# Gate and up products of the shared experts by Strassen's scheme, in an attention and mixture-of-experts block

## The chip, the cores and the metric

The kernel runs on one core of one Trainium2 chip. The metric is the device time of one launch in microseconds (us). Times of single instructions come from one profiled execution. The engines are called PE (TensorE, matrix products), DVE (VectorE), ACT (ScalarE), POOL (GpSimd) and SP (SyncE, which here only issues DMAs).

## The reference, cut to what matters

The program is one block of a transformer with adaptive layer norm: attention with 16 heads over 2048 tokens of width 512, then a feed-forward layer with 64 routed experts, four for each token, and two shared experts that see every token. All of it is float32. The change lies in the shared experts:

```python
h = _layernorm(x, axis=-1) * (1 + cb) + sb            # 2048 x 512, "flat" below
...
h = jax.nn.silu(jnp.einsum('ecd,edh->ech', xb, Wg)) * jnp.einsum('ecd,edh->ech', xb, Wu)
yb = jnp.einsum('ech,ehd->ecd', h, Wd)                # routed experts, 128 seats each
y = yb[eid, jnp.minimum(pos, CAP - 1)] * (w * valid)[:, None]
out = jnp.zeros((N, Dx), x.dtype).at[tok].add(y)
hs = jax.nn.silu(jnp.einsum('nd,sdh->nsh', flat, Sg)) * jnp.einsum('nd,sdh->nsh', flat, Su)
out = out + jnp.einsum('nsh,shd->nd', hs, Sd)         # shared experts: S = 2, HS = 512
```

Sg and Su have two shared experts of 512 hidden columns each, so 1024 hidden columns in all, over a width of 512.

## The kernel before, in words

The first two thirds of the time go to attention; nothing of it changes. After it the layer-normed tokens lie transposed in `h2T` (128 partitions, 4 chunks of the width, 2048 tokens), and the weights of the shared experts in `wsg` and `wsu`. `acc` holds the output, 16 tiles of 128 tokens.

The shared work is cut into 4 blocks `b` of 512 tokens and 8 chunks `i` of 128 hidden columns. One pair (b, i) is called a unit here. In `shared_up` a unit is two halves: the gate product and the up product, each four matmuls of 128x128 weights by 128x512 tokens, summed into one bank of PSUM (name `psg`, tag `gu`, three banks). After the second half `glu` makes silu(gate) times up: a sigmoid on ACT and two multiplies on DVE, and the result is `hs`. `shared_down` takes the eight `hs` of a block and makes the output of 128 tokens: eight matmuls of 512 columns and one add to `acc` on DVE.

The list `shared` holds all this in order: the units of a block, and after the first unit of the next block the four downs of the block before. It is used in three places, in an order written out by hand (`manual_schedule` keeps the order in which the program is written on each engine):

- The lead: the first `LEAD` = 9 halves, put between the last steps of the routing. The last of these steps writes `tok`, the table of which token sits in which expert's seat.
- The merged stage: the routed experts, step by step, are merged with the shared work by `merge`, which always takes from the list that is behind, by its columns of matmul work. For an expert, `expert_turn` transposes the gathered tokens (`load_xb` gathers them on POOL from `tok`), `expert_up` makes gate and up in one product (`pse`, also tag `gu`), `expert_mid` transposes the hidden values, and `expert_down` makes the output (`psy`), multiplies it by `gb` on DVE and writes it to memory (`ybd`). `load_expert` loads the three weights of an expert on SP's queue, into four buffers.
- The tail: the last `TAIL` = 26 entries of `shared`. Between them stands `combine`: for each tile of 128 tokens, four gathers on POOL fetch the outputs of its experts into `yg` (four buffers), and four multiply-adds on DVE put them into `acc`. `READY` sets the place of each combine by the columns of matmul work that stand before it, one tile for 3072 columns.

The tail ends with the four downs of the last block, each followed by a store of its tile.

Of the kernel before, what the change touches and what calls it, by code (L numbers as in the profile page):

```python
# [9 lines left out]
F32 = mybir.dt.float32  # L10
BF16 = mybir.dt.bfloat16
U32 = mybir.dt.uint32
AF = mybir.ActivationFunctionType
ALU = mybir.AluOpType
# [4 lines left out]
P = 128  # L19
# [4 lines left out]
def adaln_block_kernel(  # L24
# [23 lines left out]
    nc = tc.nc  # L48
    _, N, D = x.shape
    H, _, DH = Q_w.shape  # L50
    E, _, HE = Wg.shape
    S, _, HS = Sg.shape
# [4 lines left out]
    NB = N // 512  # L57
    NHC = S * HS // P
# [65 lines left out]
    with ExitStack() as att:  # L124
# [453 lines left out]
        left = []  # L578
# [362 lines left out]
    with ExitStack() as ex:  # L941
# [1 line left out]
        sgp = ex.enter_context(tc.tile_pool(name="sgp", bufs=2, side="right"))  # L943
        wdp = ex.enter_context(tc.tile_pool(name="wdp", bufs=1, side="right"))
        wts = ExitStack()
        ewp = wts.enter_context(tc.tile_pool(name="ewp", bufs=4, side="right"))
        wsd = wdp.tile([P, NHC, D], F32)
        hsh = {}
        weights = {}

        def load_expert(e):
            w = ewp.tile([P, DC, 2, HE], F32, name="wgu")
            nc.sync.dma_start(out=w[:, :, 0, :], in_=Wg[e].rearrange("(k p) h -> p k h", p=P))
            nc.sync.dma_start(out=w[:, :, 1, :], in_=Wu[e].rearrange("(k p) h -> p k h", p=P))
            wd = ewp.tile([P, D], F32, name="wd")
            nc.sync.dma_start(out=wd, in_=Wd[e])
            weights[e] = (w, wd)

        def glu(dst, pg, pu, width):

            sig = sgp.tile([P, 512], F32, name="sig")[:, :width]
            nc.scalar.activation(sig, pg, AF.Sigmoid)
            nc.vector.tensor_mul(sig, sig, pg)  # L963
            nc.vector.tensor_mul(dst, sig, pu)

        def shared_up(b, i):
            s, f = divmod(i, HS // P)
            parts = []

            def half(w):  # L970
                ps = psO.tile([P, 512], F32, name="psg", tag="gu", bufs=3)
                for k in range(DC):
                    nc.tensor.matmul(  # L973
                        out=ps,
                        lhsT=w[:, s, k, f * P : (f + 1) * P],
                        rhs=h2T[:, k, b * 512 : (b + 1) * 512],
                        start=(k == 0),
                        stop=(k == DC - 1),
                    )
                parts.append(ps)  # L980
                if len(parts) == 2:
                    hsh[b, i] = hsp.tile([P, 512], F32, name="hs")
                    glu(hsh[b, i], parts[0], parts[1], 512)

            return [(2048, lambda: half(wsg)), (2048, lambda: half(wsu))]

        def shared_down(b, i):
            t = 4 * b + i
            ps = psO.tile([P, D], F32, name="psd", tag="y")
            for f in range(NHC):  # L990
                nc.tensor.matmul(  # L991
                    out=ps,
                    lhsT=hsh[b, f][:, i * P : (i + 1) * P],
                    rhs=wsd[:, f, :],
                    start=(f == 0),
                    stop=(f == NHC - 1),
                )
            nc.vector.tensor_add(acc[:, t, :], acc[:, t, :], ps)
            if b == NB - 1:
                store(t)  # L1000
# [2 lines left out]
            nc.sync.dma_start(out=out[0, t * P : (t + 1) * P, :], in_=acc[:, t, :])  # L1003


        shared = []
        for b in range(NB):
            for i in range(NHC):
                shared += shared_up(b, i)
                if i == 0 and b > 0:  # L1010
                    shared += [(4096, lambda b=b, j=j: shared_down(b - 1, j)) for j in range(4)]
        shared += [(4096, lambda j=j: shared_down(NB - 1, j)) for j in range(4)]
        LEAD = 9
        TAIL = 4 + 2 * NHC + 4 + 2

        with tc.manual_schedule():
            nc.sync.dma_start(out=wsd, in_=Sd.rearrange("s (i p) d -> p (s i) d", p=P))
            for i in range(NHC):
                nc.gpsimd.tensor_mul(wsd[:, i, :], wsd[:, i, :], gb)
            for e in range(4):  # L1020
                load_expert(e)
            for n, (_, f) in enumerate(shared[:LEAD]):
                f()
                if n == 0:
                    turn_h(NT - 1)
                if n == 1:
                    seat_tokens(len(BLOCKS) - 2)
                if n == 1:
                    logit(NT - 1)
                    choice = choose(len(BLOCKS) - 1)  # L1030
                    next(choice)
                if n == 2:
                    next(choice)
                if n == 4:
                    positions(len(BLOCKS) - 1)
                if n == 6:
                    seat_tokens(len(BLOCKS) - 1)
        rts.close()
        xbp = ex.enter_context(tc.tile_pool(name="xbp", bufs=2))
        xbs = {}  # L1040
        xts = {}
        ups = {}
# [16 lines left out]
            nc.scalar.copy(xts[e], tp)  # L1059

        def expert_up(e):
            ps = psO.tile([P, 2 * HE], F32, name="pse", tag="gu", bufs=3)
            for k in range(DC):
                nc.tensor.matmul(  # L1064
                    out=ps,
                    lhsT=xts[e][:, k, :],
                    rhs=weights[e][0][:, k].rearrange("p i h -> p (i h)"),
                    start=(k == 0),
                    stop=(k == DC - 1),
                )  # L1070
            he = xbp.tile([CAP, HE], F32, name="he")
            glu(he, ps[:, :HE], ps[:, HE:], HE)
            ups[e] = he
# [6 lines left out]

        def expert_down(e):
            ps = psO.tile([CAP, D], F32, name="psy", tag="y")
            nc.tensor.matmul(out=ps, lhsT=hts[e], rhs=weights[e][1], start=True, stop=True)  # L1083
            y = xbp.tile([CAP, D], F32, name="y")
            nc.vector.tensor_mul(y, ps, gb)
            nc.scalar.dma_start(out=ybd[e * CAP : (e + 1) * CAP, :], in_=y)

        def expert_step(e):
            out = []

            def turn():
                if e + 3 < E:
                    load_xb(e + 3)
                expert_turn(e + 1)

            def down():
                expert_down(e - 2)
                if e + 2 < E:
                    load_expert(e + 2)

            if e + 1 < E:
                out.append((512, turn))
            if e < E:
                out.append((1024, lambda: expert_up(e)))
            if 0 <= e - 1 < E:
                out.append((128, lambda: expert_mid(e - 1)))
            if e >= 2:
                out.append((512, down))
            return out
# [22 lines left out]
        with tc.manual_schedule():  # L1132
            for e in range(3):
                load_xb(e)
            expert_turn(0)
            experts = []
            for e in range(E + 2):
                experts += expert_step(e)
            merge([experts, shared[LEAD:-TAIL]], [])
# [58 lines left out]
```

## Time and profile before

| | us |
|---|---|
| median of 3 runs | 2533.73 (2530.65 to 2536.56) |
| the profiled run | 2545.0 |
| its span | 2543.2 |
| PE, busy | 2445.4 |
| DVE, busy | 1431.6 |
| ACT, busy | 647.1 |
| the shared experts' gate and up matmuls (L973), busy | 235.4 |
| the shared experts' down matmuls (L991), busy | 111.5 |
| the routed experts' up matmuls (L1064), busy | 121.1 |
| the combines (L1126, DVE), busy | 47.8 |

The profiled run is one execution; its time stands beside its span because the rows of the trace add up to the span. "Busy" is the time in which an engine has at least one instruction in work; for PE the ends of the pipelined matmuls are modelled. A float32 matmul appears as two records of PE. The page cuts the span into 40 equal slices of 63.6 us, and gives in tenths how busy each engine is in each and what clock PE was granted. In a group's row stand the line, the engine, the operation, the tiles it writes and reads, the count, then the busy time, the mean of one in ns, and the idle time before it with what ended it. "Remote" or "unknown queue" as a releaser means that the trace doesn't show what ended a wait.

### The profile page before, as it was taken

The page shows a single profiled execution, that of the slowest core. Times are in us where ns is not written, and L with a number is a line of the kernel's source. Part 1 is how long each engine was busy: PE and PEld are TensorE (multiplying, and loading weights), DVE is VectorE, ACT ScalarE, POOL GpSimd, SP SyncE. Part 2 cuts the span into 40 slices and gives each one's busy share as a digit, 9 for nine tenths or more (in the row PEclk, how much of TensorE's full clock was granted, in tenths as well). Part 3 has the DMA queues.
Part 4 walks back from the last instruction along what each step waited for, and adds up shares of the span by engine and source line. Part 5 has one row for each costly group of instructions (what it writes and reads, how often), then busy time and mean ns, then how long its engine had stood idle before and what let it go on. Part 6 is the DMA issues. An engine that isn't in the chain of part 4 may idle for free.

```text
span 2543.2 us, 25501 instructions
## 1 busy us (share of the span) xinstructions
PE 2445.4 (96%) x8297; PEld 1484.3 (58%) x8297; DVE 1431.6 (56%) x2737; ACT 647.1 (25%) x1456; POOL 247.3 (10%) x306
## 2 busy tenths in 40 slices
PE   7999999999999999999999999989999999999989
PEld 4666666666666666666666666545444456566534
DVE  4566666666666666666666666663655522222354
ACT  3233323333232333323333333311111121211100
POOL 0000000000000000000000000040000211111163
PEclk9999999999999999999999999999999999999989
DMA  4234434444444343444444434564521467767564
GB/s 137 60 98 97 115 90 108 112 101 111 98 121 107 93 118 99 96 119 101 109 118 101 109 97 97 161 188 135 203 83 50 124 190 229 226 201 233 168 187 138
DMA packets 225420, 326.21 MB, mean 128 GB/s; under 512 B 32100, under 2 KB 140680, under 8 KB 225288
## 3 DMA queue, kind: packets, MB, share of 16 engines
q1 hardware_dynamic: 197960, 251.16, 38.2%
q0 software_dynamic: 18112, 56.64, 7.0%
q10 hardware_dynamic: 9216, 16.78, 1.7%
q8 instruction: 67, 1.10, 0.2%
q14 instruction: 65, 0.53, 0.1%
HBM read 139.91 MB, written 41.94 MB: 72 GB/s over the span
## 4 chain that ended last, share of the span: by engine, by line
PE 65%; DVE 18%; SPq 6%; issue 4%; DMA 4%; ACT 2%; another core or an unknown queue 1%; DVEq 0%; ACTq 0%; POOL 0%; POOLq 0%
PE pqk L169 12%; PE ps L408 12%; PE po L479 9%; PE psg L973 8%; DVE pt L461 6%; SPq L451 6%; PE pv L329 5%; PE pso L915 4%; PE pse L1064 4%; PE psd L991 4%; DVE nm L421 4%; DMA pt<-p 3%; DVE p L397 3%; PE psy L1083 2%; PE tpx L1057 1%
## 5 line engine op out<-in xcount | busy, mean ns | idle before, releaser
L427 ACT ACTIVATE p<-ps,nm 128x1024 f32<-128x1024 f32 (+7 forms) x384 | 332.2, 865 | 1041.4 <-DVE nm L425 368.5
L408 PE MATMUL ps<-kt,qt 128*128 128x512 f32 (+3 forms) x1280 | 536.6, 536 | 44.5 <-ACT p L427 43.6
L479 PE MATMUL po<-pt,v 128*128 128x256 f32 (+1 forms) x2304 | 568.2, 369 | 6.6 <-DVE pt L461 3.6
L479 PEld LDWEIGHTS po<-pt,v 128*128 128x128 f32 x2304 | 426.2, 191 | 221.7 <-issue 156.5
L421 DVE TENSOR_REDUCE nm<-ps 128x1 f32<-128x1024 f32 (+7 forms) x384 | 349.6, 910 | 92.2 <-PE ps L408 83.4
L461 DVE STREAM_TRANSPOSE pt<-pt 128x1664 f32<-128x1664 f32 (+2 forms) x160 | 318.0, 1988 | 66.3 <-DMA pt<-p 61.5
L408 PEld LDWEIGHTS ps<-kt,qt 128*128 128x128 f32 x1280 | 235.4, 191 | 195.4 <-issue 127.4
L420 DVE TENSOR_TENSOR ps<-ps,causal 128x128 f32<-128x128 f32 x256 | 74.5, 291 | 349.9 <-PE ps L408 349.9
L329 PE MATMUL pv<-wv,hT 128*128 128x256 f32 x1024 | 240.3, 379 | 0.0
L489 POOL DMA_DIRECT2D atd<-at x128 | 78.4, 613 | 1652.2 <-ACT at L488 1627.7
L169 PE MATMUL pqk<-hT,wq 128*128 128x512 f32 x512 | 231.5, 595 | 0.0
L169 PE MATMUL pqk<-hT,wk 128*128 128x512 f32 x512 | 231.2, 595 | 0.0
L397 DVE TENSOR_SCALAR p<-p,rs 128x1024 f32<-128x1024 f32 (+7 forms) x384 | 221.8, 606 | 9.3 <-DMA p<-atd 0.2
L329 PEld LDWEIGHTS pv<-wv,hT 128*128 128x128 f32 x1024 | 194.5, 190 | 31.4 <-issue 1.9
L915 PE MATMUL pso<-hT,v 128*128 128x512 f32 x384 | 175.5, 604 | 0.0
L169 PEld LDWEIGHTS pqk<-hT,wk 128*128 128x128 f32 x512 | 98.0, 192 | 102.3 <-issue 99.7
L169 PEld LDWEIGHTS pqk<-hT,wq 128*128 128x128 f32 x512 | 97.9, 191 | 97.3 <-issue 94.2
L973 PE MATMUL psg<-h2T,wsu 128*128 128x512 f32 x256 | 119.2, 610 | 10.4 <-DVE sig L963 10.4
L1064 PE MATMUL pse<-wgu,xbT 128*128 128x256 f32 x512 | 121.1, 379 | 0.0
L973 PE MATMUL psg<-h2T,wsg 128*128 128x512 f32 x256 | 116.2, 593 | 4.8 <-ACT h2T L750 2.8
L915 PEld LDWEIGHTS pso<-hT,v 128*128 128x128 f32 x384 | 70.7, 192 | 74.5 <-issue 73.7
L991 PE MATMUL psd<-wsd,hs 128*128 128x512 f32 x256 | 111.5, 592 | 0.0
(224 smaller groups left out, 1723.0 us busy)
## 6 DMA issues: line engine op xcount, KB each, us to landing
pt<-p SPq DMA_DIRECT2D x768, 104.0 KB
pt<-p SPq DMA_DIRECT2D x256, 124.0 KB
pt<-p SPq DMA_DIRECT2D x256, 108.0 KB
atd<-at POOLq DMA_DIRECT2D x128, 128.0 KB
wgu<-in_L_ffn_Wg_dram SPq DMA_DIRECT2D x64, 256.0 KB
wgu<-in_L_ffn_Wu_dram SPq DMA_DIRECT2D x64, 256.0 KB
wd<-in_L_ffn_Wd_dram SPq DMA_DIRECT2D x64, 256.0 KB
ybd<-y ACTq DMA_DIRECT2D x64, 256.0 KB
```

The costliest lines, as they stand in the source:

```text
L169: nc.tensor.matmul(out=ps, lhsT=w[:, k, :], rhs=hT[:, k, j * 512 : (j + 1) * 512], start=(k == 0), stop=(k == DC - 1),)
L329: nc.tensor.matmul(out=ps, lhsT=hT[:, k, t * P : (t + 1) * P], rhs=wv[:, k].rearrange("p i d -> p (i d)"), start=(k == 0), stop=(k == DC - 1),
L397: nc.vector.tensor_scalar(cols[:, :, a:b], cols[:, :, a:b], rs[:, n : n + 1], None, ALU.mult)
L408: nc.tensor.matmul(out=ps[:, o : o + wo], lhsT=q, rhs=kts[hd, (c0 + o) // 512][:, :wo], start=True, stop=True,)
L421: nc.vector.tensor_reduce(nm[:, n : n + 1], ps[:, :w], AX.X, ALU.max, negate=True)
L427: nc.scalar.activation(rows[:, r0 + c0 // P : r0 + (c0 + w) // P], ps[:, :w].rearrange("q (r b k) -> q r b k", b=4, k=32), AF.Exp, bias=nm ...
L461: nc.vector.transpose(part, part)
L479: nc.tensor.matmul(out=po if wide else po[:, P:], lhsT=vts[g][:, kt, hh * DH : (hh + 1) * DH], rhs=rows[:, r : r + last + 1 : last] if wid ...
L915: nc.tensor.matmul(out=ps, lhsT=abs_[pr][:, hd, i * P : (i + 1) * P], rhs=wo[:, hd, :], start=(hd == 0), stop=(hd == H - 1),)
L973: nc.tensor.matmul(out=ps, lhsT=w[:, s, k, f * P : (f + 1) * P], rhs=h2T[:, k, b * 512 : (b + 1) * 512], start=(k == 0), stop=(k == DC - 1),)
L991: nc.tensor.matmul(out=ps, lhsT=hsh[b, f][:, i * P : (i + 1) * P], rhs=wsd[:, f, :], start=(f == 0), stop=(f == NHC - 1),)
L1064: nc.tensor.matmul(out=ps, lhsT=xts[e][:, k, :], rhs=weights[e][0][:, k].rearrange("p i h -> p (i h)"), start=(k == 0), stop=(k == DC - 1),)
```

## The change

Gate and up of a unit, seen together, are a product of a 2 by 2 matrix of blocks with another one: the left factor has the rows gate and up and, as columns, the two halves of the width (256 each); the right factor has these two halves of the width as rows and two halves of the token block (256 tokens each) as columns. The plain way takes eight products of blocks. Strassen's scheme, in the form with shared sums, takes seven, of sums of blocks: four sums of weight blocks (`weight_sum`, per unit), four sums of token blocks (`token_sum`, per block of tokens), and seven sums of the products. All these sums are made on DVE, except one copy of a product, on ACT.

A unit is now four entries of the list, `first` to `fourth`, with two, two, two and one products. Each product is two matmuls of 256 columns, and two products share one bank of PSUM. The multiplies of `glu` move to `first` of the next unit. The first four units, in the lead, stay as they were; `LEAD` is 8 entries, and `TAIL` now holds eleven units where it held nine. The experts' `pse` leaves the tag `gu` for `pl`, which has one bank. The experts' weights are loaded by two functions into three buffers each, `load_up` right after the product that reads the buffer, and `load_down` where all three were loaded before. The tokens' sums of odd blocks go into tiles that are no longer used (`ga`, `cb`, `sb`, `parts[0]`).

```diff
-        ewp = wts.enter_context(tc.tile_pool(name="ewp", bufs=4, side="right"))
+        ewp = wts.enter_context(tc.tile_pool(name="ewp", bufs=3, side="right"))
...
-        def load_expert(e):
+        def load_up(e):
             w = ewp.tile([P, DC, 2, HE], F32, name="wgu")
             nc.sync.dma_start(out=w[:, :, 0, :], in_=Wg[e].rearrange("(k p) h -> p k h", p=P))
             nc.sync.dma_start(out=w[:, :, 1, :], in_=Wu[e].rearrange("(k p) h -> p k h", p=P))
-            wd = ewp.tile([P, D], F32, name="wd")
-            nc.sync.dma_start(out=wd, in_=Wd[e])
-            weights[e] = (w, wd)
+            weights[e] = w
+
+        def load_down(e):
+            downs[e] = ewp.tile([P, D], F32, name="wd")
+            nc.sync.dma_start(out=downs[e], in_=Wd[e])
...
+        HB = 256
...
+        def token_sum(b, j):
+
+            def quad(k, n):
+                return h2T[:, 2 * k : 2 * k + 2, b * 512 + n * HB : b * 512 + (n + 1) * HB]
...
+            if b % 2 == 0:
+                dst = tsp.tile([P, 2, HB], F32, name=f"ts{j}")
+            else:
+                dst = (ga, cb, sb, parts[0])[j - 1].rearrange("p (k n) -> p k n", k=2)
...
+            if j == 1:
+                nc.vector.tensor_sub(dst, quad(0, 1), quad(0, 0))
+            elif j == 2:
+                nc.vector.tensor_sub(dst, quad(1, 1), ts["1"])
+            elif j == 3:
+                nc.vector.tensor_sub(dst, quad(1, 1), quad(0, 1))
+            else:
+                nc.vector.tensor_sub(dst, quad(1, 0), ts["2"])
...
+        def weight_sum(n, j):
...
+            dst = wsp.tile([P, 2, P], F32, name=f"ws{j}")
+            a, b, op = {
+                1: ("21", "22", ALU.add), 2: ("1", "11", ALU.subtract),
+                3: ("11", "21", ALU.subtract), 4: ("12", "2", ALU.subtract),
+            }[j]
+            nc.vector.tensor_tensor(dst, left[a], left[b], op)
...
+        FACTORS = {
+            1: ("11", "11"), 2: ("12", "21"), 3: ("4", "22"), 4: ("22", "4"),
+            5: ("1", "1"), 6: ("2", "2"), 7: ("3", "3"),
+        }
+
+        def products(n, js):
+            ps = psO.tile([P, 2, HB], F32, name="pst", tag="gu", bufs=3)
+            for h, j in enumerate(js):
+                left, right = FACTORS[j]
+                w, x_ = units[n][left], tsets[UNITS[n][0]][right]
+                for k in range(2):
+                    nc.tensor.matmul(
+                        out=ps[:, h], lhsT=w[:, k, :], rhs=x_[:, k, :],
+                        start=k == 0, stop=k == 1,
+                    )
+            return [ps[:, h] for h in range(len(js))]
+
+        def first(n):
+            u = unit(n)
+            p1, p6 = products(n, (1, 6))
+            u["p1"] = sgp.tile([P, HB], F32, name="p1")
+            nc.scalar.copy(u["p1"], p1)
+            u["u"] = sgp.tile([P, HB], F32, name="u", bufs=1)
+            nc.vector.tensor_add(u["u"], u["p1"], p6)
+            while glus:
+                glus.pop()()
+
+        def second(n):
+            u = units[n]
+            p7, p5 = products(n, (7, 5))
+            u["v"] = sgp.tile([P, HB], F32, name="v", bufs=1)
+            nc.vector.tensor_add(u["v"], u["u"], p7)
...
+            nc.vector.tensor_add(u["up"][:, HB:], u["v"], p5)
+            nc.vector.tensor_add(u["u"], u["u"], p5)
+            for j in (1, 2, 3):
+                weight_sum(n + 1, j)
+
+        def third(n):
+            u = units[n]
+            p4, p3 = products(n, (4, 3))
+            nc.vector.tensor_add(u["up"][:, :HB], u["v"], p4)
+            nc.vector.tensor_add(u["g"][:, HB:], u["u"], p3)
+            weight_sum(n + 1, 4)
+
+        def fourth(n):
+            u = units[n]
+            (p2,) = products(n, (2,))
+            nc.vector.tensor_add(u["g"][:, :HB], u["p1"], p2)
+            sig = sgp.tile([P, 512], F32, name="sig512")
+            nc.scalar.activation(sig, u["g"], AF.Sigmoid)
...
+            def finish():
+                nc.vector.tensor_mul(sig, sig, u["g"])
+                nc.vector.tensor_mul(hsh[b, i], sig, u["up"])
+
+            glus.append(finish)
+            if b + 1 < NB:
+                for j in {4: (1, 2), 5: (3,), 6: (4,)}.get(i, ()):
+                    token_sum(b + 1, j)
...
+        LEAD = 8
         shared = []
...
+        for i in range(LEAD // 2):
+            shared += shared_up(0, i)
+        UNITS = [(b, i) for b in range(NB) for i in range(NHC)][LEAD // 2 :]
+        for n, (b, i) in enumerate(UNITS):
+            for c, f in ((1024, first), (1024, second), (1024, third), (512, fourth)):
+                shared.append((c, lambda n=n, f=f: f(n)))
+            if i == 0 and b > 0:
+                shared += [(4096, lambda b=b, j=j: shared_down(b - 1, j)) for j in range(4)]
         shared += [(4096, lambda j=j: shared_down(NB - 1, j)) for j in range(4)]
-        LEAD = 9
-        TAIL = 4 + 2 * NHC + 4 + 2
+        TAIL = 4 + 4 * NHC + 4 + 12
...
-            for e in range(4):
-                load_expert(e)
+            for e in range(3):
+                load_up(e)
+                load_down(e)
...
-            ps = psO.tile([P, 2 * HE], F32, name="pse", tag="gu", bufs=3)
+            ps = psO.tile([P, 2 * HE], F32, name="pse", tag="pl", bufs=1)
...
+            if e + 3 < E:
+                load_up(e + 3)
...
                 expert_down(e - 2)
-                if e + 2 < E:
-                    load_expert(e + 2)
+                if e + 1 < E:
+                    load_down(e + 1)
...
             expert_turn(0)
+            for j in range(1, 5):
+                weight_sum(0, j)
+                token_sum(0, j)
```

## The prediction

> **What bounds the kernel now.** I read the busy time and the slices of the page first: which engine is full, and where that changes.
>
> ```profile
> PE 2445.4 (96%) x8297; PEld 1484.3 (58%) x8297; DVE 1431.6 (56%) x2737; ACT 647.1 (25%) x1456; POOL 247.3 (10%) x306
> ...
> PE   7999999999999999999999999989999999999989
> ...
> DVE  4566666666666666666666666663655522222354
> ...
> PEclk9999999999999999999999999999999999999989
> ```
>
> TensorE (PE) is full from end to end, at full clock. VectorE (DVE) is at a fifth while the experts run (slices 32 to 37), and rises in the last two. The change touches only slices 32 to 40, so next I read the table of stages: the last piece of the lead (2017 to 2024), experts merged with shared work (to 2408), and the tail in four pieces: three shared halves, four downs, the other halves, the last four downs.
>
> ```profile
> core 0: us, PE busy (x) PEld busy (x) DVE busy (x) ACT busy (x) POOL busy (x), PEclk, DMA share, GB/s
> 2016.90:2023.90 7.00, 7.00 (x21) 3.12 (x19) 1.80 (x4) 0.41 (x1) 2.94 (x3) 1.00 0.32 90
> 2023.90:2408.30 384.40, 384.40 (x1390) 232.13 (x1389) 111.31 (x237) 77.28 (x211) 57.77 (x61) 1.00 0.67 208
> 2408.30:2420.30 12.00, 12.00 (x30) 5.30 (x29) 4.51 (x7) 1.19 (x2) 6.31 (x6) 1.00 0.44 123
> 2420.30:2447.70 27.40, 27.40 (x65) 12.13 (x64) 15.65 (x22) 0.00 (x0) 21.10 (x21) 1.00 0.67 196
> 2447.70:2511.60 63.90, 51.46 (x113) 22.28 (x112) 38.35 (x54) 4.07 (x7) 40.35 (x38) 0.89 0.67 205
> 2511.60:2543.20 31.60, 27.66 (x65) 11.97 (x63) 6.35 (x9) 0.00 (x0) 0.00 (x0) 0.97 0.11 41
> ```
>
> In the merged stage PE never waits and DVE has 273 us free. The tail differs: from 2447.7 to 2511.6 DVE works 38 of 64 us, as all 64 gathers of expert outputs are combined there. The groups by shape give the durations:
>
> ```profile
> L1064 PE MATMUL pse<-wgu,xbT 128*128 128x256 f32 x512 | 121.1, 379 | 0.0
> ...
> L973 PE MATMUL psg<-h2T,wsu 128*128 128x512 f32 x256 | 119.2, 610 | 10.4 <-DVE sig L963 10.4
> ...
> L1126 DVE SCALAR_TENSOR_TENSOR acc<-yg,wk,acc 128x512 f32<-128x512 f32 x64 | 47.8, 752 | 5.2 <-DMA yg<-ybd,slot 3.6
> ...
> L336 DVE TENSOR_TENSOR v<-pv,vb 128x256 f32<-128x256 f32 x128 | 52.5, 410 | 47.6 <-PE pv L329 47.5
> ...
> L964 DVE TENSOR_TENSOR hs<-sig,psg 128x512 f32<-128x512 f32 x32 | 22.0, 688 | 41.5 <-PE psg L973 38.9 <-issue 2.0
> ```
>
> Finally the timeline of DVE in the tail, for how closely its instructions follow each other:
>
> ```profile
> 2427.34 0.69 DVE L998 TENSOR_TENSOR acc<-acc,psd 128x512 f32<-128x512 f32 x1 [5.09 <-PE psd L991]
> 2427.94 6.13 DVE L1126 SCALAR_TENSOR_TENSOR acc<-yg,wk,acc 128x512 f32<-128x512 f32 x8
> 2434.20 0.69 DVE L998 TENSOR_TENSOR acc<-acc,psd 128x512 f32<-128x512 f32 x1
> 2434.81 1.57 DVE L1126 SCALAR_TENSOR_TENSOR acc<-yg,wk,acc 128x512 f32<-128x512 f32 x2
> ```
>
> An instruction that doesn't need the one before starts 0.08 us before that one's end (2434.81 after 2434.20 + 0.69). In the four combines of a tile each needs the one before and starts 0.035 after its end: the eight of two tiles in 6.13 us are six steps of 0.787, one of 0.668 and the last one's 0.75. So a 128x256 sum costs DVE 0.326 us, or 0.445 if the next reads it.
>
> **The own time.** The profiled run took 2545.0 us, 1.8 around the span of 2543.2. It holds a stall: DVE stood from 2446.9 to 2463.6 with the releaser unknown, PE then waited 0.57, 1.51 and 10.36 us for it, and eight matmul records took 6.51 instead of 3.60 at half clock after it: 15.3 us. Without it 2529.7; the median of the runs, 2533.7, is 4.0 above. So the timed runs hold at most a part of that stall.
>
> **The change, part by part.**
>
> *TensorE.* A matmul is two records, 0.429 us from start to start at 512 columns and 0.216 at 256 (L329, L479 and L1064 alike, with the 0.19 us weight loads inside). A unit (one of 32 pairs of token block and hidden chunk) costs 8 x 2 x 0.429 = 6.86 us before and 7 x 2 x 2 x 0.216 = 6.05 after. 28 of 32 units change: 28 x 0.81 = 22.7 us less. Bounds: 24 if 256 columns took exactly half; 20 if they took L1064's busy time (0.2365).
>
> *VectorE, per unit.* Added: four weight sums and seven sums of products, all 128x256; v and the first weight sum are read at once: 9 x 0.326 + 2 x 0.445 = 3.82. The two 128x512 multiplies stay: 0.72 + 0.60. Together 5.15 where it was 1.32. Token sums: four of 0.61 for each of four blocks. ScalarE gets one copy of 0.365 (as L488), hidden in its 80% of idle time.
>
> *Merged stage.* 17 units, 8 downs and all experts. Before, it held 37 halves; the work of three halves (10.3 us) moves to the tail, and 17 x 0.81 = 13.8 goes: 384.4 becomes 360. DVE rises from 111 us to 111 + 17 x 3.8 + 5 = 181 of 360: half. Between two chunks of a unit stand about 2 us of expert matmuls, so three buffers of products give 11 us for DVE's work on a chunk (2.3 us at most), and the weight sums, made after chunk two, are wanted 6 us later. Hidden; without the experts between, it is what happens in the tail. The single bank for the experts' products (tag pl, once free after routing) needs sigmoid and two multiplies between two experts: 0.2 + 0.28 + 0.6 = 1.1 us, against 1.4 us of PE work that stands between them at the closest; hidden, up to 2 us lost over the stage if DVE is late.
>
> *Expert weights.* The issues on SP stay three per expert. load_up(e+3) waits for the up product of e, load_down(e+1) for the down of e-2, and behind each wait stand only the next loads. Each comes about three expert steps (5.6 us each) before its use; before, the up weights had under two, and PE waited 0.4 us for them in all. Nothing.
>
> *Lead.* LEAD falls from 9 halves to 8. The last half (3.43 us) covered the first gather of tokens: POOL issues it at 2019.0, a gather's data are used 3.3 us after its issue at the earliest (2412.37 to 2415.70 in the tail), and PE now comes at 2020.45. It waits to 2022.4, and 0.9 for the second (issued at 2020.36): +2.8. The eight first sums of DVE (4 us) run beside that. The 3.43 us of work is done later and is in the sum.
>
> *Tail.* Eleven units instead of nine: PE work 11 x 6.05 + 8 x 6.86 + 0.7 (last add) = 122.1, against 117.3 before. But no expert stands between the chunks, and DVE combines 16 tiles at 3 x 0.787 + 0.67 = 3.03 each, placed by columns: three by the fourth unit, six in the downs, seven in units five to ten.
> - Units 1 to 4: DVE 4 x 5.15 + 1.2 (token sums) + 3 x 3.03 = 30.9; PE has 24.2 and leaves 1.5 before DVE's end: 29.5.
> - Four downs: PE 27.5; DVE 20.6, hidden.
> - Units 5 to 11: DVE still owes the last add and two tiles (6.7), then 7 x 5.15 - 1.3 + 7 x 3.03 = 56; less 1.5 at the end: 61. In each unit DVE itself waits for the product it has just freed a buffer for, or for the sigmoid (0.6): I take 0.7, so 66. PE has 42.4.
> - Last downs 27.5 + 0.7; their first seven matmuls hide the last multiplies.
> Sum 151, so 29 over PE's own work. Bounds: 24 (no waits inside DVE) to 37 (no overlap, below). Gathers: 64 at 1.4 us are there after some 96 us, well before their combines; their buffers now lie partly where the experts' tiles lay, whose last readers are the writes of expert outputs that the first gather waits for in any case.
>
> *Two rules.* The Trainium skill, "VectorE: DVE Perf Modes", section "The DRAIN you can't avoid", says the next op doesn't start until the pipe is empty, with an exception for ops that aren't held[...]. The row (0.61 for 0.69) says the exception holds here. By the rule each 256 sum costs 0.41 or more: 0.75 more per unit, 8 more in the tail. I follow the row.
> "TensorE: Matmul & The Clock Gate", section "A second HAM failure mode: psum-queue depth-cycling", speaks against this change: short idles between groups of matmuls make the clock fall to half and back. The row: 0.89 in the stage with the 10.4 us wait, 1.00 in all without one. In units 5 to 11 PE would be busy 64%, with waits up to 3 us where a tile's combine lies before a freed buffer; by the row few windows halve, and PE has slack: +3. By the rule, halved throughout, PE needs 85 for 66: +19.
>
> Sum: -22.7 + 2.8 + 29 + 3 = +12. From 2529.7 this gives 2542; the 4.0 that the timed runs hold on top I keep by half, since a tail that DVE bounds covers late gathers: **2544**.
>
> **Rivals.**
> - *DVE stays hidden in the tail too*: -22.7 + 2.8, 2514. For it: DVE's share is 56%, and three product buffers. It decides where a unit plus its tile costs DVE less than PE's 6.05; I count 5.15 + 3.03 = 8.2, so sums would have to cost 0.13, not 0.33. Against it: DVE already worked 38 of 64 us there.
> - *The loss is half as large and cancels the gain*: sums nearer 0.30, no half clock, and the runs' 4 us vanish: -22.7 + 2.8 + 20 - 2, about 2532.
> - *The clock halves through units 5 to 11*: the rule above, 13 to 19 on top: 2560.
> - *The change doesn't do what it says* (256 columns gain nothing) is out: three lines show 0.216.
>
> **How the numbers follow.** Chances: likeliest 0.62 (its own range 2535 to 2554), hidden 0.10, cancelled 0.16, half clock 0.12. A measurement can tell about 0.2%, 5 us. Slower: 0.58 of the first and the last, 0.02 of the cancelled: 0.72. Same: 0.15, faster 0.13. The range leaves out the hidden case and the end of the last: 2527 to 2560.
>
> **What would show it.** PE busy for the 11 tail units with gaps of 1 to 3 us released by DVE sums; none of them in the merged stage; that stage near 360 us; 2 to 3 us before the first expert transpose; the tail near 150 us; PEclk under 1 in its second half. A tail under 130 us would make me wrong by the DVE sum, PE waits among the experts by the cover.

## The result and the profile after

The changed kernel takes 2541.15 us (2537.05 to 2544.97, five runs). The kernel before, timed beside it, takes 2531.37 (2530.65 to 2536.56, five runs). The ratio is 1.0037, with a 95% interval of 1.0023 to 1.0050, so 9.8 us slower: clear of noise, but small. The forecast was 2544, slower. The profiled run is the fastest of the five: 2537.05 us, its span 2535.3.

The page of the changed kernel, busy time and slices:

```profile
PE 2425.5 (96%) x8633; PEld 1550.1 (61%) x8633; DVE 1551.0 (61%) x3061; ACT 658.4 (26%) x1484; POOL 253.6 (10%) x306
...
PE   7999999999999999999999999979999899999988
...
DVE  4566666666666666666666666663655653644775
...
PEclk9999999999999999999999999989999999999999
```

PE is busy 20 us less than before and DVE 119 more. DVE stood at 2 of 10 in slices 33 to 37 and now stands at 3 to 6; in slices 38 and 39 it is at 7, where it was at 3 and 5. PE's row hardly tells: its 8 in slice 39 was there before too, from the stall. So the stages follow: the merged stage, units 1 to 4 of the tail, its four downs, units 5 to 11, the last downs.

```profile
core 0: us, PE busy (x) PEld busy (x) DVE busy (x) ACT busy (x) POOL busy (x), PEclk, DMA share, GB/s
2018.20:2374.90 356.70, 356.70 (x1557) 264.36 (x1556) 178.55 (x425) 82.55 (x224) 61.20 (x61) 1.00 0.75 225
2374.90:2407.70 32.80, 27.45 (x115) 22.55 (x114) 29.15 (x64) 3.68 (x8) 21.18 (x20) 0.95 0.56 168
2407.70:2435.20 27.50, 27.50 (x66) 12.17 (x65) 18.00 (x27) 0.63 (x1) 21.41 (x21) 1.00 0.72 211
2435.20:2503.70 68.50, 52.60 (x198) 41.57 (x197) 61.65 (x123) 5.83 (x13) 26.90 (x25) 0.88 0.45 138
2503.70:2535.30 31.60, 27.60 (x65) 11.94 (x63) 4.61 (x8) 0.63 (x1) 0.00 (x0) 0.99 0.09 34
```

Among the experts PE is busy in every microsecond and DVE in half of them. In units 5 to 11 it is the other way round: DVE is busy 61.65 of 68.5 us, while PE, busy 52.6 by the profile, waits. PE's timeline there names whom it waits for (the brackets hold the wait ahead of the instruction and what ended it):

```profile
2442.51 2.06 PE L1062 MATMUL pst<-h2T,wsg 128*128 128x256 f32 x4 [1.98 <-DVE u L1074]
...
2459.80 1.13 PE L1062 MATMUL pst<-silc,wsu 128*128 128x256 f32 x4 [1.70 <-DVE g L1100]
...
2468.44 1.13 PE L1062 MATMUL pst<-sb,ws 128*128 128x256 f32 x4 [2.82 <-DVE g L1094]
...
2485.26 1.13 PE L1062 MATMUL pst<-h2T,wsg 128*128 128x256 f32 x4 [2.93 <-DVE u L1086]
...
2494.57 2.08 PE L1062 MATMUL pst<-h2T,wsg 128*128 128x256 f32 x4 [2.93 <-DVE u L1086]
```

Nine such waits in units 5 to 11 sum to 15.9 us, three in units 1 to 4 to 5.35; five of the twelve are shown. Each is a product that wants the bank `pst` which a sum on DVE has yet to read. What DVE does in that time is seen in its timeline over one unit:

```profile
2460.71 0.42 DVE L1074 TENSOR_TENSOR u<-p,pst 128x256 f32<-128x256 f32 x1 [0.96 <-ACT p L1072]
2461.05 0.68 DVE L1107 TENSOR_TENSOR sig<-sig,g 128x512 f32<-128x512 f32 x1
2461.76 0.69 DVE L1108 TENSOR_TENSOR hs<-sig,up 128x512 f32<-128x512 f32 x1
2462.38 0.41 DVE L1082 TENSOR_TENSOR v<-u,pst 128x256 f32<-128x256 f32 x1
2462.82 0.42 DVE L1085 TENSOR_TENSOR up<-v,pst 128x256 f32<-128x256 f32 x1
2463.16 0.41 DVE L1086 TENSOR_TENSOR u<-u,pst 128x256 f32<-128x256 f32 x1
2463.49 0.42 DVE L1048 TENSOR_TENSOR ws<-wsu 128x256 f32<-128x256 f32 x1
...
2464.62 3.11 DVE L1265 SCALAR_TENSOR_TENSOR acc<-yg,wk,acc 128x512 f32<-128x512 f32 x4
2467.65 0.41 DVE L1093 TENSOR_TENSOR up<-v,pst 128x256 f32<-128x256 f32 x1
2467.98 0.41 DVE L1094 TENSOR_TENSOR g<-u,pst 128x256 f32<-128x256 f32 x1
...
2470.01 0.42 DVE L1074 TENSOR_TENSOR u<-p,pst 128x256 f32<-128x256 f32 x1 [0.96 <-ACT p L1072]
```

From `u` to `u` a unit lasts 9.30 us, where PE needs 6.05. A combine of 3.11 us stands between the weight sums and the sums of chunk three, and PE's wait of 2.82 ahead of 2468.44 ends with the sum `g` (L1094), which was queued behind it.

Counted from the start of the lead, 1986.6 us in this profile and 1993.2 in that of before, to the end, the changed kernel takes 548.7 us against 534.7 (the stall of 15.3 us in before's profile taken off): 14.0 more. The timed runs differ by 9.8 (5.8 to 12.7 by the interval). The 4 us between the two figures can't be placed: ahead of the lead, where the code is the same, these two profiles already differ by 6.6 us, and the lead began between 1986.6 and 1997.6 us in all profiles of this study. A stage below is therefore measured inside its profile, and a kernel by the median of its runs.

### The profile page after: what moved, and what is told of

It is laid out like the page before. It is cut to its first block, busy times and chain, and to the rows that moved or that the text cites. A ratio compares the mean times of both kernels' runs of the same rounds, so it can differ in the third digit from the quotient of the medians.

```text
span 2535.3 us, 26583 instructions
## 1 busy us (share of the span) xinstructions
PE 2425.5 (96%) x8633; PEld 1550.1 (61%) x8633; DVE 1551.0 (61%) x3061; ACT 658.4 (26%) x1484; POOL 253.6 (10%) x306
## 4 chain that ended last, share of the span: by engine, by line
PE 61%; DVE 21%; SPq 6%; issue 5%; DMA 4%; ACT 2%; POOL 0%; DVEq 0%; ACTq 0%; POOLq 0%
PE pqk L169 12%; PE ps L408 11%; PE po L479 9%; DVE pt L461 7%; SPq L451 6%; PE pv L329 5%; PE pst L1062 5%; PE pse L1201 4%; PE psd L1122 4%; PE pso L915 4%; DVE nm L421 4%; DMA pt<-p 3%; DVE p L397 3%; PE psy L1222 2%; DVE acc L1265 1%
## 5 line engine op out<-in xcount | busy, mean ns | idle before, releaser
L1201 PEld LDWEIGHTS pse<-wgu,xbT 128*128 128x128 f32 x512 | 93.6, 190 | 12.1 <-issue 1.4
L1184 POOL DMA_INDIRECT xb<-h2d,tok x64 | 66.0, 1031 | 280.7 <-PE tpx L1194 266.7
```

The source lines that it names most:

```text
L1201: nc.tensor.matmul(out=ps, lhsT=xts[e][:, k, :], rhs=weights[e][:, k].rearrange("p i h -> p (i h)"), start=(k == 0), stop=(k == DC - 1),)
```

## The experiments

Runs 1 to 4, 5 to 8 and 9 to 12 each shared a chip and their runs of the kernel before: medians 2530.99, 2543.31 and 2532.04 us. The chip of runs 5 to 8 differs in a way told at the end, which is why two of its kernels were run again. My theory: DVE's work bounds the tail, above all where a combine lies in a unit; the scheme itself gains what it promises where experts stand between the products. The rivals: the clock halved by PE's waits costs the time; the new loads or the single bank cost it; the sums also cost something among the experts.

**1. The scheme among the experts only.** The 18 units of the merged stage change, the tail keeps the plain halves, and the lead is ten halves.

```diff
-        LEAD = 8
+        LEAD = 10
...
+        UNITS = [(b, i) for b in range(NB) for i in range(NHC)][5 : 2 * NHC + 7]
```

> The seven-product units stand only in the merged stage, 18 of them, from the sixth unit of block 0 to the seventh of block 2; the five units of the lead (ten halves) and the nine of the tail are plain. My theory (the cover of the experts hides every VectorE sum, and the loss comes from the tail alone): 18 x 0.81 = 14.6 us under the kernel before, about 2517, with no wait of TensorE on VectorE between 2025 and 2390. Rival (the sums, the single bank of the experts' products or the split loads cost time among the experts too): 2525 or more, with such waits in the merged stage.

Measured: 2516.46 us, ratio 0.9940 (0.9927 to 0.9954), so 14.5 less than before. Its merged stage of 364.8 us holds no wait of PE, with DVE busy 183.3. The full saving of 18 x 0.81 us arrives: the scheme is not at fault where there is other PE work between its products. The new loads and the bank are in this kernel too, but the interval (11.6 to 18.5 us less) is too wide to say that they cost nothing.

**2. The scheme in the tail only.** The lead and the merged stage keep the plain halves.

```diff
-        LEAD = 8
+        LEAD = 9
...
+        UNITS = [(b, i) for b in range(NB) for i in range(NHC)][2 * NHC + 5 :]
```

> The complement: lead (nine halves) and merged stage plain, seven-product units only in the tail, the same eleven as in the changed kernel. My theory: the tail lasts some 155 us where its plain work takes 130.8 (eleven units of 6.86, eight downs, the last add), so about 24 us over the kernel before, 2555. Rival (the tail loses little and the loss of the changed kernel sits elsewhere): under 2540.

Measured: 2556.92 us, ratio 1.0097 (1.0082 to 1.0113), so 25.9 more than before. PE's waits from the tail's start to the end of its trace:

```profile
PE pst L1062 <- DVE u L1086: 9.3, 6, 2.9
PE pst L1062 <- DVE g L1094: 6.3, 3, 2.9
PE pst L1062 <- DVE g L1100: 3.4, 2, 1.7
PE pst L1062 <- DVE u L1074: 2.0, 1, 2.0
```

(us in all, times, longest.) These are 21.0 us, all for DVE. The tail lasts 155.7 us (2400.4 to 2556.1), where PE's own work is 122.1. With the waits that leaves 12.6 us, in which products behind a wait ran slower: the granted clock is 0.92 over this stretch. Whether the slow clock costs anything beside the waits is asked in runs 7 and 12. Runs 1 and 2 together, -14.5 and +25.9, make +11.4; the whole change measured +9.8. So, within the intervals, the loss lies in the tail alone.

**3. Only the split loads and the single bank**, in the kernel before.

```diff
-        ewp = wts.enter_context(tc.tile_pool(name="ewp", bufs=4, side="right"))
+        ewp = wts.enter_context(tc.tile_pool(name="ewp", bufs=3, side="right"))
...
-            ps = psO.tile([P, 2 * HE], F32, name="pse", tag="gu", bufs=3)
+            ps = psO.tile([P, 2 * HE], F32, name="pse", tag="pl", bufs=1)
...
+            if e + 3 < E:
+                load_up(e + 3)
```

> The kernel before with nothing of the seven products, but with the experts' weights in split buffers of three and the experts' products in a bank of their own. My theory: no difference, 2531 within 4 us; TensorE stays full in the merged stage. Rival (the single bank makes TensorE wait for the sigmoid and the multiplies of each expert): up to 64 x 0.3 = 19 us more, with waits before the experts' up products.

Measured: 2534.00 us, ratio 1.0011 (1.0005 to 1.0018): 3.0 more, a small but real loss. The trace shows 0.9 us of it as waits ahead of `pse` (0.7 for the transposed tokens, 0.2 for a PE instruction), and its merged stage is 1.4 us longer than before's (385.8 against 384.4, from the first transpose to the end of the last `psy`). The rest I could not place. The changed kernel's own merged stage has no such wait.

**4. A longer lead.** Ten halves in place of eight, the rest as changed.

```diff
-        LEAD = 8
+        LEAD = 10
...
-                for j in {4: (1, 2), 5: (3,), 6: (4,)}.get(i, ()):
+                for j in {5: (1, 2, 3), 6: (4,)}.get(i, ()):
```

> The changed kernel with ten plain halves in the lead instead of eight, so 27 seven-product units instead of 28. My theory: the wait of 2.7 and 0.5 us before the first expert's transposes goes, at 0.8 us for the unit that is plain again: 2.4 us under the changed kernel, about 2539. Rival (the first sums on VectorE delay the gathers wherever they stand): the wait stays above 2 us and the time at 2541 or more.

Measured: 2537.01 us, ratio 1.0025 (1.0017 to 1.0033), some 3 us better than the changed kernel's 1.0037, though the two intervals overlap. What the traces show for certain is the wait. The first transposes of the two traces, of the changed kernel:

```profile
2016.64 0.63 PE L1194 MATMUL tpx<-ident,xb 128*128 128x128 f32 x4 [2.72 <-DVE ts L1022]
2017.79 0.66 PE L1194 MATMUL tpx<-ident,xb 128*128 128x128 f32 x4 [0.52 <-DMA xb<-h2d,tok]
```

and with the longer lead:

```profile
2020.55 1.04 PE L1194 MATMUL tpx<-ident,xb 128*128 128x128 f32 x8
```

The waits of 2.72 and 0.52 us are gone, because PE comes later: the gathers are issued as slowly as before (1.42 and 1.50 us, see the end).

**5. Small combines.** Each multiply-add of a combine works on 8 of its 512 columns, so most of the routed experts' output is left out; the gathers stay whole.

```diff
-                    acc[:, t, :], yg[:, k, :], wk[:, n : n + 1], acc[:, t, :], ALU.mult, ALU.add
+                    acc[:, t, 8 * k : 8 * k + 8], yg[:, k, 8 * k : 8 * k + 8], wk[:, n : n + 1],
+                    acc[:, t, 8 * k : 8 * k + 8], ALU.mult, ALU.add
```

> The changed kernel with each combine of an expert's output done on 8 of 512 columns (most of the routed experts' part of the output is left out); gathers, stores and their order stay. My theory: VectorE's bill per tail unit falls from 8.2 us to 5.8 at most, under TensorE's 6.05, so the tail falls from 155 to 122 to 130 us: 2541 becomes 2508 to 2516, and the waits of TensorE on VectorE sums in the tail nearly vanish. Rival (the chain of products, sums and sigmoid within a unit, or the clock, sets the tail): the time stays above 2530.

Measured: 2541.91 us, ratio 0.9994 (0.9986 to 1.0002). The expectation failed. Its trace has waits that no other kernel had shown me but the profile of before:

```profile
ACT p L1072 <- remote: 36.6, 3, 26.6
...
DVE acc L1129 <- remote: 14.7, 1, 14.7
```

ACT waited 26.6 us and DVE 14.7, both until 2450, with the releaser unknown. So this run doesn't measure the combines alone.

**6. Small combines in the kernel before**, the same edit and the same part left out.

> The kernel before with the same cut, combines on 8 of 512 columns (the rest of the routed part is left out). My theory: VectorE did not bound its tail, so no more than the rests of stalls go: 2526 to 2531. Rival (the combines bound both tails): 20 us or more less.

Measured: 2549.14 us, ratio 1.0018 (1.0008 to 1.0028): slower, against the expectation. Waits of unknown releaser again (DVE 21.5 us at once for an add of the downs, ACT 20.7 in two), and PE stood 11.5 us behind that add. Within this chip the changed kernel with small combines is 7.2 us faster than the old one with small combines, but both hold such waits, so this doesn't price the scheme.

**7. Extra work for PE in the tail.** One more product of 256 columns, which nobody reads, ahead of each of the 44 groups of products in the tail: 19 us of PE time. If the half clock sets the tail's length, keeping PE busy wins it back.

```diff
         def products(n, js):
+            if n >= len(UNITS) - 11:
+                fill = psO.tile([P, HB], F32, name="fill", tag="tr")
+                nc.tensor.matmul(out=fill, lhsT=wsg[:, 0, 0, 0:P], rhs=h2T[:, 0, 0:HB], start=True, stop=True)
```

> The changed kernel with one idle 256-column matmul more (into a bank that nothing reads) ahead of each of the 44 groups of products in the tail: 44 x 0.43 = 19 us of TensorE work. My theory (VectorE sets the pace of the tail's units, TensorE has slack): 0 to 4 us more, 2541 to 2545, with fewer stretches at half clock. Rival (TensorE's own time or its clock sets the pace): 19 us more, 2560.

Measured: 2561.17 us, ratio 1.0068 (1.0054 to 1.0082): a miss as well. PE waited 12.5 us in four places for an unknown releaser ahead of the extra products.

**8. The weight sums of the merged stage twice.** Each sum of 16 units is made a second time into the same tile.

```diff
             nc.vector.tensor_tensor(dst, left[a], left[b], op)
+            if 0 < n < len(UNITS) - 11:
+                nc.vector.tensor_tensor(dst, left[a], left[b], op)
```

> The changed kernel with each weight sum of the merged stage's units made twice: some 64 sums, 64 x 0.33 = 21 us of VectorE work more among the experts. My theory (hidden there): no difference from the changed kernel, 2541 within 3 us. Rival (VectorE is on the path in the merged stage too): 10 to 21 us more.

Measured: 2549.46 us, ratio 1.0024 (1.0014 to 1.0033), no more than the changed kernel's 1.0037; but the changed kernel was not timed on this chip, so the trace has to decide. Its tail has a wait of unknown releaser too (10.3 us), its merged stage has none (columns as in the stage table):

```profile
2023.00:2380.00 357.00, 357.00 (x1549) 264.19 (x1548) 201.98 (x489) 79.72 (x222) 60.69 (x60) 1.00 0.76 225
```

DVE has 64 instructions and 23 us more than in the changed kernel, and PE is busy throughout all the same. The sums are hidden there, with room to spare.

**10. The changed kernel again**, on the chip of the last four runs.

> The changed kernel unaltered, beside the three others on the same chip, since the kernel before took 2531 us in one set of runs and 2543 in another. If that set's chip posts TensorE's finished products late while gathers run densely (the stall in the trace of before), the changed kernel, whose combines are paced by VectorE, may stand nearer to the kernel before there: ratio 0.998 to 1.002; on the other kind 1.0037, as measured. Rival (the 12 us are a slower chip in every part): 1.0037 on both.

Measured: 2542.21 us, ratio 1.0041 (1.0026 to 1.0056).

**11. Small combines again** (the edit of 5), on this chip.

> The changed kernel with combines on 8 of 512 columns (most of the routed part of the output is left out), run again. My theory (VectorE's bill sets the tail, and the late posts took the gain away in the first try): where no wait with an unknown releaser shows, 22 to 30 us under the unaltered changed kernel; where such waits show, their sum is missing from that. Rival (the chain within a unit sets the tail): within 8 us of the changed kernel, without such waits.

Measured: 2515.86 us, ratio 0.9932 (0.9917 to 0.9947), 26.4 less than run 10. There is no wait of unknown releaser now. Units 1 to 4 and units 5 to 11:

```profile
2385.80:2410.70 24.90, 24.25 (x111) 20.50 (x110) 22.05 (x58) 3.04 (x7) 15.86 (x15) 1.00 0.56 161
...
2438.20:2485.00 46.80, 44.29 (x197) 36.26 (x196) 40.09 (x122) 5.71 (x13) 27.66 (x27) 1.00 0.69 214
```

Units 5 to 11 take 46.8 us instead of 68.5, at full clock, with PE busy 95%. Sums and combines together don't fit beside PE's 6.05 us a unit. The sums alone nearly do: a unit here still lasts 6.83 us from `u` to `u` (2447.89 to 2454.72), of which the small combine takes some 0.6 and a wait of DVE 0.96. Run 9 has units with no combine at all.

**12. Extra work for PE again** (the edit of 7).

> The changed kernel with 44 idle 256-column matmuls, 19 us of TensorE work, in the tail's units, beside the changed kernel itself. My theory (TensorE has slack there): 0 to 5 us over the changed kernel. Rival (TensorE's own time sets the pace): 15 to 19 us over it.

Measured: 2546.48 us, ratio 1.0060 (1.0046 to 1.0075), 4.3 more than run 10. Units 5 to 11 of run 10:

```profile
2446.10:2513.30 67.20, 51.09 (x198) 40.57 (x197) 60.63 (x121) 5.82 (x13) 26.86 (x25) 0.90 0.46 141
```

and with the extra products:

```profile
2443.50:2510.30 66.80, 58.46 (x253) 48.24 (x252) 60.21 (x119) 5.71 (x13) 25.76 (x24) 0.97 0.45 138
```

The clock rises from 0.90 to 0.97, PE's busy time by 7 us, and the length stays. DVE's busy time is the same in both. From the lead's start to the end the two profiles differ by 0.4 us (550.4 in run 10, 550.8 here). The intervals of the two ratios overlap, and the 4.3 of the medians are not found in this stage.

**9. The combines moved to the downs.** As run 4, and the 16 tiles get places written out by hand: three in unit 4 or right after it, four in the first downs, one each in units 7 and 10, seven from the end of unit 11 on through the last downs. (READY holds how many tiles are combined by each entry of the tail, AT the entries at which that rises.)

```diff
-            READY = []
...
-                READY.append(max(0, cols * 4 // (3 * 4096) - 1))
+            AT = {13: 1, 15: 3, 16: 4, 17: 6, 18: 7, 31: 8, 41: 9, 47: 11, 48: 13, 49: 15, 50: 16}
+            READY = [max([0] + [u for m, u in AT.items() if m <= n]) for n in range(len(tail))]
```

> The changed kernel with ten halves in the lead, and the combines taken from between the tail's units and put where VectorE has room: three by the end of the fourth unit, four in the first four downs, two among the last seven units, seven beside the last four downs. Nothing is left out. My theory (a unit alone costs VectorE 5.15 us, under TensorE's 6.05; unit plus combine is what sets the tail): the saving of 27 x 0.81 = 22 us comes through but for 5, so 12 to 20 us under the kernel before, ratio 0.992 to 0.995. Rival (units of seven products bound by VectorE or their chain even without combines): ratio 1.000 or more.

Measured: 2512.25 us (2510.01 to 2517.52), ratio 0.9929 (0.9914 to 0.9944): 19.8 less than before and 30 less than run 10. It beats both kernels. Its tail, in the four pieces:

```profile
2374.90:2399.40 24.50, 24.33 (x110) 20.38 (x109) 21.55 (x50) 3.06 (x8) 15.49 (x15) 1.00 0.54 155
2399.40:2426.90 27.50, 27.50 (x66) 12.21 (x65) 24.74 (x39) 0.63 (x1) 19.81 (x18) 1.00 0.65 190
2426.90:2476.60 49.70, 45.23 (x197) 37.77 (x196) 41.34 (x95) 5.71 (x13) 20.36 (x21) 0.97 0.42 124
2476.60:2508.20 31.60, 27.64 (x65) 11.98 (x63) 24.81 (x36) 0.63 (x1) 13.76 (x12) 1.00 0.60 197
```

DVE now works 24.7 us beside the first downs and 24.8 beside the last ones, where it had 18 and 4.6. PE needs little of DVE there (one add for each down), and is busy throughout the first. One wait of any size is left:

```profile
2470.51 1.13 PE L1062 MATMUL pst<-sb,ws 128*128 128x256 f32 x4 [2.82 <-DVE g L1094]
```

It lies beside one of the two combines left in units 5 to 11. The units without a combine show what bounds them next. PE passes two of them at its own 6.05 us (12.1 us from 2432.05 to 2444.14, busy throughout), but DVE takes 6.34 from `u` to `u`, with a wait in each:

```profile
2435.54 0.42 DVE L1074 TENSOR_TENSOR u<-p,pst 128x256 f32<-128x256 f32 x1 [0.95 <-ACT p L1072]
...
2441.88 0.42 DVE L1074 TENSOR_TENSOR u<-p,pst 128x256 f32<-128x256 f32 x1 [0.95 <-ACT p L1072]
```

So the sums fit beside PE's 6.05 only without this wait; with it DVE falls behind by some 0.3 us a unit. The next section says where it comes from.

A rival is that the kernel before would gain as much from moving its combines. That kernel was not run so; but in run 1, whose tail is plain, PE's waits from the merged stage to the end are 1.8 us in all, so little is to be gained there. Of the 30 us under run 10, some 3 to 4 are the longer lead's: 3 by run 4, and 4.4 by run 10's own profile (a wait of 2.8 us and a slow stretch of 2.4 behind it, less 0.8 for the unit that is plain again).

## Why the prediction was right, point by point

The direction, the place and the mechanism held; the time came out 2.9 us under the forecast, and that it came so near is in part luck, as the last points say. The sum of the parts, set against pieces of the changed kernel's profile:

| step | predicted | measured |
|---|---|---|
| a unit on PE, unstalled | 6.05 | 6.04 (2380.95 to 2386.99) |
| merged stage | 360 | 360.0 (first transpose to last `psy`) |
| DVE busy in it | 181 of 360 | 178.6 of 356.7 |
| lead: waits for the tokens | 1.9 + 0.9 | 2.72 + 0.52 |
| units 1 to 4 | 29.5 | 31.1 |
| four downs | 27.5 | 27.5 |
| units 5 to 11 | 66, and 3 for the clock | 68.5 |
| last downs and add | 28.2 | 28.3 |
| change from the lead on | +12 | +14.0 |
| change of the run | +10.3 (2544) | +9.8 |

- *The saving on PE* is as predicted; run 1 shows it by itself (18 x 0.81 = 14.6, measured 14.5).
- *The merged stage hides DVE's work.* Shown three times: no wait of PE there in the changed kernel (but for the first tokens), in run 1, and in run 8 with 23 us more on DVE.
- *DVE bounds the tail, through the combines.* Shown by taking them away (run 11: 26.4 us, against the predicted excess of 29) and by moving them (run 9: 30, some 3 to 4 of them by the longer lead). The price of a sum, 0.33 us or 0.445 where the next reads it, is what the timeline shows (2462.82 to 2463.16; 2462.38 to 2462.82). The Trainium skill's rule in "VectorE: DVE Perf Modes", "The DRAIN you can't avoid", taken at its general form, would have put 0.41 or more there; the row was right, and the exception that the same section makes holds.
- *Units 5 to 11*: the 61 us of DVE work were right (61.65). The term that was off is the idle time inside DVE: I took 0.7 us a unit and it is 6.85 in seven, 1.0. Of this 4.8 are five waits of 0.96 for ACT's copy of the first product (L1072), which I had costed as hidden because ACT is idle most of the time. The product was not late. In the unit shown PE began it at 2454.33, over 6 us ahead of DVE's sum:

```profile
2454.33 1.13 PE L1062 MATMUL pst<-h2T,wsg 128*128 128x256 f32 x4 [0.89 <-DVE u L1086]
...
2459.34 0.41 DVE L1100 TENSOR_TENSOR g<-p,pst 128x256 f32<-128x256 f32 x1
2459.78 0.63 ACT L1102 ACTIVATE sig<-g 128x512 f32<-128x512 f32 x1 [8.48 <-DVE g L1100]
2460.32 0.35 ACT L1072 COPY p<-pst 128x256 f32<-128x256 f32 x1
2460.71 0.42 DVE L1074 TENSOR_TENSOR u<-p,pst 128x256 f32<-128x256 f32 x1 [0.96 <-ACT p L1072]
```

  The copy is written behind the sigmoid of the unit before, and that sigmoid (L1102) waits for DVE's last sum `g`. So DVE waits for ACT, which had waited for DVE: 1.37 us from `g` to `u`, the same in run 11 (2453.35 to 2454.72) and in run 9 (2440.51 to 2441.88). Where a combine lay between `g` and `u` (2496.89), no wait is left. A copy written ahead of the sigmoid should take this wait out; no run tried it.
- *Units 1 to 4*: 1.6 us over the 29.5. I took no idle time of DVE there; it waited 2.5 us for the same copy.
- *The clock*: 3 us were added for it, and that step failed. The clock did fall as the Trainium skill's "TensorE: Matmul & The Clock Gate", section "A second HAM failure mode: psum-queue depth-cycling", has it (0.88 in units 5 to 11), but run 12 restores it to 0.97 without a gain. PE had the slack. The rival that the clock sets the tail, 13 to 19 us more, falls with the same run. Its 19 took PE for halved throughout; the section speaks of a clock that goes to and fro, and that is what the trace shows.
- *The lead*: 3.24 us for 2.8, and run 4 gets about 3 back. The prediction called the first sums of DVE harmless there. They may not be: POOL's issues of the first two gathers took longer beside them (below), and the tokens came 4.6 us after the first issue instead of the 3.3 that I had read off a gather in the tail. The trace names DVE's sum as what ended PE's wait, but that sum had ended 0.7 us earlier; the slower gather as the cause is inferred.
- *The loads and the bank for nothing*: in the kernel before they cost 3.0 us (run 3), half of it unplaced. In the changed kernel no wait for them appears, so whether they cost anything there stays open.
- *Half of the 4.0 us* by which before's runs stood above its profile without the stall was kept, which took 2542 to 2544. In the five runs beside the changed kernel before stood 1.7 above (2531.4 against 2529.7); why is not known. The near hit is partly luck: the terms that were too small (1.6 in units 1 to 4, some 2 for DVE's idle time, 0.4 in the lead) were met by the 3 for the clock that cost nothing. The stages of the profile give +14.0, so 2543.7 from 2529.7, and the runs gave 2541.15.
- *Slips in the working* that change nothing: DVE's fifth is in slices 33 to 37, not 32; the last downs too stood under full clock (0.97) without a wait of PE; and the lower bound of 20 us on PE's saving holds only if the old matmuls are priced by their busy time as well.
- *Hidden in the tail* and *cancelled*, the faster rivals: both fall by the stage table. The first becomes true when the combines move to the downs: run 9's 2512 is what that rival gave (2514), and it decides where it said, at DVE's work per unit under PE's 6.05.

## What to carry to other kernels

A scheme that trades matrix work for vector work is priced stage by stage, at the unit in which both engines hand buffers to each other: here 0.81 us saved against 3.8 us added was worth all of its 0.81 where other matrix work stood between, and worth less than nothing where 3 us of another vector job came into the same 6 us. When a vector engine becomes the bound of a stage, look for a neighbouring stage in which the matrix engine needs nothing from it, and move the unrelated vector work there before giving the scheme up. A copy on an idle engine still has a price if, in that engine's order, it stands behind an instruction that waits for a busy one: look at what is written ahead of it, not only at the engine's idle share.

## What the runs showed of the hardware that was not expected

On one chip (runs 5 to 8; before took 2543 us there and 2531 to 2532 on the two others), and in the profile of before, DVE and ACT were released late, by something the trace does not show, while gathers were being issued one after the other. In before's profile DVE waited up to 16.7 us so; in run 5 the longest wait was 26.6 us (ACT), in run 6 21.5. These three ended when POOL had stopped issuing, 4 to 6 us after the start of the last gather of a dense row: last gather at 2458.48, DVE and ACT on at 2463.57 and 2463.66; in run 5 2445.67 and 2450.12; in run 6 2446.11 and 2451.73. Neither the changed kernel's trace nor those of runs 1 to 4 and 9 to 12 have such a wait in the tail, though gathers stand in rows there too. The cause stays open: thinner gathers were not tried on that chip.

POOL's issues of the tokens' gathers, in the changed kernel:

```profile
2012.04 1.42 POOL L1184 DMA_INDIRECT xb<-h2d,tok  x1 [11.17 <-issue]
2013.76 1.50 POOL L1184 DMA_INDIRECT xb<-h2d,tok  x1 [0.30 <-issue]
```

The same issues took 1.03 and 0.96 us before. They lie beside DVE's first weight and token sums, which read two operands from SBUF; the fourth and fifth in the same profile, without such sums beside them, take 0.94 and 0.95. Runs 4, 10, 11 and 12 have the same 1.42 and 1.50. That the sums are the cause is inferred.

Waits of 2 to 3 us are enough to halve PE's clock for a while, but not every one does: in the changed kernel stretches of 3.4 or 6.8 us at half clock begin at 2401.6, 2442.6, 2469.9 and 2493.8, within or just after waits of 2.82, 1.98, 2.82 and 2.93 us; the wait of 2.93 ahead of 2485.26 brought none. In the profiles of runs 10, 11 and 12 the wait in the lead brought such a stretch of 6.8 us into the merged stage, which was 2.3 to 2.5 us longer for it (362.3 to 362.5 against 360.0): there PE has no slack, and the slow clock counts.
